# A Hawk and RWKV block on one core: each recurrent gate by fifteen products

## The chip, the cores and the metric

The kernel runs on one core of a Trainium2 chip. The metric is the device time of one execution in microseconds; smaller is better. TensorE multiplies matrices into PSUM, which is eight banks of 128 x 512 numbers here; ScalarE (ACT) applies functions and copies; VectorE (DVE) does element-wise work, scans and statistics; GpSimd (POOL) does element-wise work between SBUF tiles; SyncE (SP) issues DMAs. Each engine works through its own instructions in program order, and waits on semaphores where it needs another's result.

## What is computed

Eight sequences of 1024 tokens with 256 channels go through a layer norm, and a recurrent block (Hawk) and a feed-forward block (RWKV channel mix) are added to the input. Everything is float32.

```python
gate = xn @ Wg.T;  u = xn @ Wi.T                       # 256 -> 384
y  = causal_depthwise_conv(u, conv_w, K=4) + conv_b
ig = sigmoid(y @ lru_Wi.T + lru_bi)                    # 384 -> 384
rg = sigmoid(y @ lru_Wg.T + lru_bg)
alpha = exp(-8 * softplus(lam) * rg)
beta  = sqrt(1 - alpha**2 + 1e-6)
h[t]  = alpha[t] * h[t-1] + (beta * ig * y)[t]
hawk  = (gelu(gate) * h) @ Wo.T                        # 384 -> 256
xr = mu_r * xn + (1 - mu_r) * xn_prev;  xk likewise with mu_k
ffn = sigmoid(xr @ W_r.T) * (relu(xk @ W_k.T)**2 @ W_v.T)
out = x + hawk + ffn
```

## The kernel before

Channels lie on partitions, tokens along the free axis: 384 channels are three chunks of 128, 1024 tokens are two halves of 512, so that one 128 x 512 product fills a PSUM bank. The kernel does not multiply block by block. A 2 x 2 block of weights (two output chunks, two input chunks) times two token halves takes seven products instead of eight. The class `Group` holds such a set. It uses sums of weight blocks, which `weight_sum` makes once on GpSimd, and sums of token blocks, which `token_sum` (L803) makes on GpSimd, four for each matrix that is multiplied. Of a group's steps, `seed` (L491) copies bank A to a new bank B, `five` (L496) copies bank C to SBUF, `fork_c` (L499) and `fork_d` (L507) add B and that copy on VectorE, and `evict` applies the output function. Where a third input chunk exists, each of the four outputs gets one more ordinary product, eleven a group in all.

The groups of a sequence are: u0, u1, u2 (u and gate, 7 products each, L415), k (7, L415), r and v (7 each, by token, L421), o (11, by token, L421), and l0, l1, l2 for the two recurrent gates together (11 each, L415): the six rows of output chunks of both gates are taken as three pairs. A product by token is four instructions of 128 columns. In the last sequence l takes the same chunk of both gates as a pair, and the o products of the last two sequences are done there without groups (L830). In the first sequence u0 and v are plain as well.

Around them, per sequence: VectorE adds three of the four convolution taps (`conv_rest`, L898; the first tap, `conv_first`, is ScalarE's), mixes xk and xr (`mix`, L820), computes layer-norm statistics of the next sequence (L725, L729), transposes its tokens in 32 x 32 squares (L780), which sixteen small DMAs on SP's queue (`spread`) carry to their places; and for the recurrence computes 1 - alpha squared (`decay_rest`, L915), `gated_input` (L922), `scaled_input` (L925), the scan `recur` (L930) and `gated_state` (L934). ScalarE normalizes, evicts, and computes exp, square and sqrt. `add_x` is a DMA on GpSimd's queue that adds x to the sum in `side`.

The order of instructions is laid out by hand. Every step is entered with a time by `at` or `pe`, all steps are sorted by it, and the sorted list is issued. For steps of ScalarE, VectorE, GpSimd and SP the table `PLACES` (four parts: first, second, middle, last sequence) replaces the time by one that a planner found, relative to the start of the sequence; TensorE's products count up a clock of their own in the order in which the loop calls `Group.step`. So the table fixes only an order, and what each engine waits for at run time is the data. Banks are taken from the front of a list of eight and given back at its end.

The recurrence of a sequence runs while the next sequence's u, k and r products are made; its o product comes later in that sequence. The two gates stand at the end of each sequence, and the u products of the next one are interleaved with their last groups.

Of the kernel before, what the change touches and what calls it, by code (L numbers as in the profile page):

```python
# [12 lines left out]
P = 128  # L13
NT = 512
# [22 lines left out]
        "early weight_sum u 0 False": 2.01, "early_put 1": 2.2, "early normalize 4 1": 2.3,  # L37
        "early weight_sum u 2 False": 2.32, "early normalize_on_vector 5": 2.35,
        "early weight_sum u 1 False": 3.04, "early weight_sum u 3 False": 3.59, "early_put 2": 3.62,
        "early normalize 6 1": 3.64, "early normalize_on_vector 7": 3.65, "u0_0 evict 0 0": 3.66,  # L40
        "early parameters": 4.36, "early weight_sum r 2 False": 4.66, "u0_0 evict 1 0": 5.16,
        "early weight_sum r 0 False": 5.38, "early weight_sum k 0 False": 5.75,
        "early weight_sum k 2 False": 6.13, "early weight_sum k 1 False": 6.5, "early load 0 8": 6.86,
        "early_put 3": 6.86, "early weight_sum r 1 False": 6.87, "early weight_sum k 3 False": 7.18,
        "early mix_before k 0": 7.48, "early token_sum x 0": 7.5, "early weight_sum r 3 False": 8.66,
        "early mix_before k 1": 8.7, "early mix k 0": 9.03, "u0_0 evict 1 1": 9.92,
        "early token_sum x 1": 10.53, "u1 seed": 10.86, "u0_0 evict 0 1": 11.55, "early mix k 1": 11.69,
        "u1 five": 12.23, "u2 seed": 12.91, "early token_sum x 2": 13.19, "second stats 1 1": 13.5,
        "conv_first 1": 13.59, "second stats 2 1": 14.23, "early token_sum k 0": 14.35,
        "early mix_before r 0": 14.94, "second stats 6 1": 14.96, "early token_sum x 3": 15.51,  # L50
        "u1 fork_c": 15.86, "u1 evict A 0 0": 16.16, "early token_sum k 1": 16.67,
        "second stats 0 1": 16.67, "u2 five": 16.85, "early mix_before r 1": 17.53,
        "early token_sum k 2": 17.84, "u2 fork_c": 17.86, "second stats 7 1": 18.67, "k seed": 18.86,
        "early token_sum k 3": 19.0, "conv_first 0": 19.55, "early mix r 0": 20.16, "k five": 20.89,
        "u1 fork_d": 21.66, "early token_sum r 0": 21.82, "u1 evict C 0 1": 21.86,
        "second stats 3 1": 22.46, "early halve v": 22.98, "u2 fork_d": 23.19,
        "second stats 4 1": 23.99, "u2 evict A 0 0": 24.04, "early weight_sum l 0 False": 24.71,
        "second stats 5 1": 24.72, "u2 evict C 0 1": 24.73, "k evict A 0 0": 25.41,
        "early constant 16": 25.61, "k fork_c": 25.86, "early constant 0": 26.09,
        "early mix r 1": 26.69, "r seed": 26.86, "early constant 1": 27.54, "u1 late": 27.8,  # L60
        "conv_rest 1 1": 28.18, "r five": 28.48, "conv_first 2": 29.16, "early token_sum r 1": 29.68,
        "u2 evict B 1 0": 30.51, "conv_rest 0 1": 30.84, "u1 evict B 1 0": 31.19, "u2 late": 31.87,
        "early token_sum r 2": 32.34, "k fork_d": 32.34, "early constant 2": 33.49,
        "early token_sum r 3": 33.63, "early weight_sum l 1 False": 33.7, "r fork_c": 33.77,
        "early constant 3": 34.38, "early weight_sum l 3 False": 34.51, "k evict B 1 0": 34.53,
        "early weight_sum l 2 False": 35.77, "r fork_d": 35.86, "k late": 36.28, "conv_rest 2 1": 36.43,
        "conv_rest 1 2": 38.21, "r evict B 1 0": 39.35, "k evict C 0 1": 40.03, "conv_rest 0 2": 40.08,
        "deviation": 40.1, "r evict A 0 0": 41.42, "conv_rest 0 3": 41.48, "inverse 0 8": 41.6,
        "r evict C 0 1": 42.02, "conv_rest 2 2": 42.96, "normalize 4 1": 43.4, "token_sum y 0": 44.45,
        "r late": 44.8, "conv_rest 1 3": 45.6, "l0 seed": 46.8, "conv_rest 2 3": 47.0, "l0 five": 47.65,  # L70
        "normalize 2 1": 47.7, "normalize 7 1": 47.72, "normalize 1 1": 47.74, "normalize 6 1": 48.0,
        "normalize 5 1": 48.29, "value 0": 48.34, "token_sum y 1": 48.34, "normalize 0 1": 48.93,
        "value 6": 49.06, "token_sum y 2": 49.38, "l0 evict A 0 0": 49.72, "value 2": 49.8,
        "normalize 3 1": 50.52, "token_sum y 3": 50.52, "l0 fork_c": 50.86,
        "early weight_sum o 0 False": 51.6, "early weight_sum v 2 False": 51.62,
        "early weight_sum o 1 False": 51.64, "value 4": 51.67, "early weight_sum v 0 False": 51.68,
        "l1 seed": 51.86, "early weight_sum o 2 False": 52.06, "early weight_sum v 1 False": 52.44,
        "early constant 4": 52.82, "add_x": 52.82, "l1 five": 52.86, "early constant 5": 53.14,
        "early constant 6": 53.47, "early constant 7": 53.79, "l0 fork_d": 53.98,
        "early weight_sum v 3 False": 54.65, "early constant 8": 55.03,  # L80
        "early weight_sum o 3 False": 55.21, "early constant 9": 55.59, "l0 evict C 0 1": 55.86,
        "early constant 10": 55.91, "early constant 11": 56.23, "early constant 12": 56.43,
        "put_transposed 0 0": 56.46, "early constant 13": 56.56, "early constant 14": 56.88,
        "put_transposed 1 0": 56.94, "early constant 15": 57.03, "early constant 17": 57.35,
        "put_transposed 0 1": 57.51, "early constant 18": 57.67, "load_for_squares": 57.86,
        "put_transposed 1 1": 58.19, "token_sum x 0": 58.36, "mix_before k 0": 58.88,
        "token_sum x 2": 59.52, "l0 evict B 1 0": 60.1, "mix k 0": 60.68, "mix_before k 1": 60.9,
        "l1 evict A 0 0": 62.13, "token_sum x 1": 62.18, "l1 fork_c": 62.86, "decay 0": 62.93,
        "token_sum k 0": 63.34, "l0 evict D 1 1": 64.27, "mix k 1": 64.5, "l2 seed": 65.07,
        "l2 five": 65.86, "token_sum x 3": 66.0, "mix_before r 0": 66.55, "l1 fork_d": 66.86,  # L90
        "token_sum k 2": 67.17, "mix r 0": 67.6, "mix_before r 1": 67.77, "token_sum k 1": 68.33,
        "l1 evict C 0 1": 69.0, "token_sum k 3": 69.63, "decay_square 0": 69.8, "l2 evict A 0 0": 70.91,
        "l2 fork_c": 71.0, "mix r 1": 71.2, "decay_rest 0": 71.31, "decay 1": 71.71, "stats 1 1": 72.2,
        "stats 6 1": 72.5, "stats 2 1": 72.8, "decay 2": 73.05, "l1 evict B 1 0": 74.39,
        "l1 evict D 1 1": 75.19, "l2 fork_d": 75.92, "decay_square 2": 75.99, "stats 4 1": 76.1,
        "stats 0 1": 76.2, "stats 7 1": 76.72, "decay_square 1": 77.1, "stats 5 1": 77.45,
        "l2 evict C 0 1": 78.21, "stats 3 1": 79.6, "decay_rest 1": 83.35, "decay_rest 2": 86.75
    },
    "second": {
        "token_sum r 0": -0.6, "gated_input 0": 0.68, "u0 seed": 1.51, "token_sum r 2": 2.1,  # L100
        "gated_input 1": 3.27, "beta 0": 3.69, "token_sum r 1": 4.69, "u0 five": 4.92,
        "u0 evict A 0 0": 5.6, "u0 fork_c": 6.66, "token_sum r 3": 6.66, "l2 evict B 1 0": 7.78,
        "scaled_input 0": 7.82, "u1 seed": 8.58, "l2 evict D 1 1": 9.27, "recur 0 L": 10.06,
        "u1 five": 10.07, "k seed": 10.75, "k five": 11.43, "gated_input 2": 11.51, "u0 fork_d": 12.94,
        "beta 1": 13.61, "recur 0 R": 13.74, "u0 evict C 0 1": 14.84, "scaled_input 1": 15.2,
        "u1 evict A 0 0": 15.52, "beta 2": 16.21, "u1 fork_c": 16.62, "k evict A 0 0": 17.43,
        "k fork_c": 17.43, "conv_first 0": 18.12, "gated_state 0": 18.23, "u2 seed": 19.46,
        "scaled_input 2": 19.65, "u0 evict B 1 0": 20.14, "u2 five": 20.83, "token_sum o 0": 21.08,
        "u1 fork_d": 21.36, "deviation": 21.51, "conv_first 1": 21.89, "recur 2 L": 22.24,
        "u1 evict C 0 1": 23.23, "k fork_d": 23.7, "recur 2 R": 24.5, "u1 late": 25.41,  # L110
        "inverse 0 8": 25.96, "k late": 26.1, "conv_rest 0 1": 26.33, "u2 evict A 0 0": 26.78,
        "k evict C 0 1": 27.46, "u2 fork_c": 27.83, "gated_state 2": 28.63, "k evict B 1 0": 29.25,
# [129 lines left out]
def kernel(  # L242
# [211 lines left out]
    def now():  # L454
        return clock[0]
# [907 lines left out]
```

## Time and profile before

| what | value |
|---|---|
| time, median of 3 runs | 619.85 us (619.23 to 619.87) |
| profiled execution: span from first to last instruction | 617.3 us (the page gives no other time for it; 2.6 us below the median) |
| TensorE busy | 611.9 us, 99% |
| VectorE busy | 530.7 us, 86% |
| ScalarE busy | 472.6 us, 77% |
| GpSimd busy | 319.4 us, 52% |
| HBM read and written | 19.94 MB and 8.39 MB |
| granted TensorE clock | 1.000 |

The page shows one execution. Busy time is the union of an engine's instructions; their records overlap by some 0.09 us from one to the next, so the distance between starts is shorter than a record. A float32 product is two records (MATMUL), so a count of 288 is 144 products.

### The profile page before, as it was taken

To read this page: it belongs to the slowest core of one execution; us is meant where nothing else is said; L and a number is where in the kernel's file an instruction comes from. 1 tells how busy PE (TensorE), PEld (TensorE's weight loads), DVE (VectorE), ACT (ScalarE), POOL (GpSimd) and SP (SyncE) were. 2 spreads that over 40 slices of the span, in tenths; PEclk is the share of its full clock that TensorE was granted. 3 is DMA by queue.
4 is the path that set the end of the run, shared out by engine and by line. 5 is a ranking of instruction groups with operands and counts; after the bars stand their busy time and mean duration, and the time that the engine had idled before them with its cause. 6 is when DMAs were issued, how large, how long until landed. Compare 5 with 4: busy or idle time off the path is not lost.

```text
span 617.3 us, 7489 instructions
## 1 busy us (share of the span) xinstructions
PE 611.9 (99%) x2539; PEld 369.8 (60%) x2539; DVE 530.7 (86%) x659; ACT 472.6 (77%) x671; POOL 319.4 (52%) x227
## 2 busy tenths in 40 slices
PE   8999999999999999999999999999999999999997
PEld 5475445954469544794448844497445964457466
DVE  5898798999989788898899888998888986789696
ACT  5988998569894788938888398884898749884880
POOL 4977913578044950649307482085911769427000
PEclk9999999999999999999999999999999999999999
DMA  8201600164002910039000480006500044000403
GB/s 274 67 1 13 124 0 1 31 175 69 0 1 52 202 21 1 0 82 193 0 1 1 102 171 1 1 6 159 110 0 1 18 120 70 0 0 1 70 17 119
DMA packets 35479, 35.10 MB, mean 57 GB/s; under 512 B 2801, under 2 KB 34929, under 8 KB 35441
## 3 DMA queue, kind: packets, MB, share of 16 engines
q1 hardware_dynamic: 26416, 25.63, 15.1%
q0 software_dynamic: 8320, 8.39, 9.2%
q10 hardware_dynamic: 704, 0.60, 0.3%
q8 instruction: 20, 0.33, 0.2%
q14 instruction: 19, 0.15, 0.1%
HBM read 19.94 MB, written 8.39 MB: 46 GB/s over the span
## 4 chain that ended last, share of the span: by engine, by line
PE 96%; DVE 3%; issue 1%; ACT 0%; DVEq 0%
PE bank L415 67%; PE bank L421 22%; PE bank L830 4%; DVE y L898 1%; PE bank L581 1%; PE bank L1025 1%; DVE xk L780 0%; PE bank L1044 0%; DVE bank L499 0%; PE bank L754 0%; DVE q L930 0%; DVE side L507 0%; DVE five L507 0%; DVE bank L507 0%; ACT xt L749 0%
## 5 line engine op out<-in xcount | busy, mean ns | idle before, releaser
L415 PE MATMUL bank<-y,w_l 128*128 128x512 f32 x288 | 138.2, 593 | 0.1
L898 DVE SCALAR_TENSOR_TENSOR y<-u,par,y 128x1024 f32<-128x1024 f32 x72 | 112.5, 1586 | 0.2
L491 ACT COPY bank<-bank 128x512 f32<-128x512 f32 x76 | 43.7, 576 | 60.7 <-PE bank L415 44.9
L415 PEld LDWEIGHTS bank<-y,w_l 128*128 128x128 f32 x288 | 53.0, 190 | 59.2 <-issue 56.6
L499 DVE TENSOR_TENSOR bank<-bank,five 128x512 f32<-128x512 f32 x76 | 52.3, 690 | 26.8 <-PE bank L415 24.9
L415 PE MATMUL bank<-ysum,sum_l 128*128 128x512 f32 x144 | 71.0, 593 | 0.0
L415 PE MATMUL bank<-xsum,sum_u 128*128 128x512 f32 x138 | 69.4, 592 | 0.0
L803 POOL TENSOR_TENSOR tr<-g 128x512 f32<-128x512 f32 x12 | 22.0, 1835 | 83.4 <-ACT u L611 69.4
L803 POOL TENSOR_TENSOR ysum<-y,ysum 128x512 f32<-128x512 f32 x16 | 28.4, 1777 | 53.5 <-DVE y L898 51.0
L803 POOL TENSOR_TENSOR xsum<-ysum 128x512 f32<-128x512 f32 x12 | 15.0, 1270 | 66.0 <-PE bank L421 58.8
L415 PEld LDWEIGHTS bank<-ysum,sum_l 128*128 128x128 f32 x144 | 26.9, 190 | 34.8 <-issue 29.2
L496 ACT COPY five<-bank 128x512 f32<-128x512 f32 x76 | 43.6, 583 | 4.8 <-PE bank L415 2.9
L415 PE MATMUL bank<-xnT,w_u 128*128 128x512 f32 x92 | 47.0, 592 | 0.0
L415 PEld LDWEIGHTS bank<-xsum,sum_u 128*128 128x128 f32 x138 | 25.7, 190 | 29.6 <-issue 26.8
L623 ACT ACTIVATE tr<-bank,half_b 128x512 f32<-128x512 f32 x48 | 31.9, 678 | 14.5 <-PE bank L415 14.4
L421 PE MATMUL bank<-w_o,g 128*128 128x128 f32 x288 | 37.0, 275 | 0.0
L623 ACT ACTIVATE ti<-bank,half_b 128x512 f32<-128x512 f32 x48 | 31.5, 683 | 7.1 <-PE bank L415 6.9
L421 PEld LDWEIGHTS bank<-w_o,g 128*128 128x128 f32 x288 | 35.0, 192 | 2.9 <-issue 2.9
L749 ACT ACTIVATE xt<-xt,mv,std 128x256 f32<-128x256 f32 x60 | 33.9, 597 | 0.9 <-DVE mv L740 0.9
L922 DVE SCALAR_TENSOR_TENSOR ti<-ti,y 128x1024 f32<-128x1024 f32 (+1 forms) x25 | 29.9, 1217 | 3.9 <-ACT ti L623 3.9
L803 POOL TENSOR_TENSOR ysum<-y 128x512 f32<-128x512 f32 x16 | 20.3, 1270 | 23.7 <-DVE y L898 16.3
L925 DVE SCALAR_TENSOR_TENSOR ti<-ti,q 128x1024 f32<-128x1024 f32 (+1 forms) x25 | 31.8, 1272 | 0.7
(165 smaller groups left out, 1476.2 us busy)
## 6 DMA issues: line engine op xcount, KB each, us to landing
side<-in_x_dram POOLq DMA_DIRECT2D x8, 1024.0 KB, 9.3
xt<-in_x_dram SPq DMA_DIRECT2D x28, 256.0 KB, 5.0
xnT<-xk SPq DMA_DIRECT2D x96, 64.0 KB, 2.0
out_dram<-side SPq DMA_DIRECT2D x12, 512.0 KB, 5.2
xt<-in_x_dram SPq DMA_DIRECT2D x1, 1024.0 KB, 5.5
out_dram<-side SPq DMA_DIRECT2D x4, 256.0 KB, 2.2
out_dram<-side SPq DMA_DIRECT2D x6, 128.0 KB, 1.7
w_l<-in_lru_wg_dram SPq DMA_DIRECT2D x1, 576.0 KB, 6.1
```

The costliest lines, as they stand in the source:

```text
L415: nc.tensor.matmul(banks[b], weight, tokens, start=start, stop=True, skip_group_check=True)
L421: nc.tensor.matmul(banks[b][:, p], tokens[:, p], weight, start=start and j == 0, stop=True, skip_group_check=True,)
L491: nc.scalar.copy(banks[bank["B"]], banks[bank["A"]])
L496: nc.scalar.copy(self.five, banks[bank["C"]])
L499: nc.vector.tensor_tensor(banks[bank["C"]], banks[bank["B"]], self.five, ALU.add)
L623: nc.scalar.activation(dst[:, m, HALVES[h]], src, AF.Tanh, bias=half_b[:, b + m : b + m + 1], scale=0.5)
L749: nc.scalar.activation(xa, xa, AF.Identity, bias=m, scale=r)
L803: nc.gpsimd.tensor_tensor(dst[o], a, b, ALU.subtract)
L830: nc.tensor.matmul(banks[b][:, j * D : (j + 1) * D], lhs[:, c, (t + j) * P : (t + j + 1) * P], families[w][:, c, :], start=(j == 0 and c = ...
L898: nc.vector.scalar_tensor_tensor(y[:, m, :], u[:, m, k : k + S], column(COL_CONV_W + k * HC + m), y[:, m, :], ALU.mult, ALU.add,)
L922: nc.vector.scalar_tensor_tensor(ti[:, m, p], ti[:, m, p], 1.0, y[:, m, p], ALU.add, ALU.mult)
L925: nc.vector.scalar_tensor_tensor(ti[:, m, p], ti[:, m, p], 0.5, q[:, m, p], ALU.mult, ALU.mult)
```

## The change

Each recurrent gate is now computed on its own: three output chunks by three input chunks by two token halves, 18 block products, are done by fifteen. Two gates take 30 products a sequence, where l0, l1 and l2 took 33. `gate_weight` makes the fifteen weight operands for both gates at once, in twenty steps (18 on GpSimd, one on ScalarE, one on VectorE) in the first sequence, out of the raw weights, which are loaded into the tile q. `form` makes ten sums of y blocks on VectorE, into the six halves of u (whose values the convolution has used up) and the four parts of ysum; five of the fifteen products take y itself. GpSimd's four sums of y are gone. Partial sums are shared between the outputs through three bank copies (`copy`) and four copies into the output's own place in tr or ti (`keep`), on ScalarE, and five adds (`join`) on VectorE, for each gate.

The order of all engines, TensorE and SP included, now comes from a new table `PLACES` (1,182 entries) with the starts of the sequences in `BASES`; every step has an entry of its own, the products too. The sums for o go to q where they went to tr. The copies `five` take a buffer from a list and give it back. Stores are steps of their own. The groups u, k, r, v and o, the convolution, the recurrence and the output are computed as before.

```diff
-        "l": fixed("w_l", [HC, 2 * HC * P]),
...
-    def l_group(s, gi):
...
+    def gates(name, n, s):
+        dst = (tr, ti)[n]
...
+        rows = {**raw_forms(s), **{i: forms(s)[k] for i, k in FORM_OF.items()}}
...
+        def mm(i, key, new=False):
+            if new:
+                bank[key] = take()
+            product(bank[key], gate_w[:, i, n, :], rows[i], start=new)
+        def copy(key, new):
+            bank[new] = take()
+            nc.scalar.copy(banks[bank[new]], banks[bank[key]])
+        def keep(key, o, h):
+            nc.scalar.copy(place(o, h), banks[bank[key]])
...
+        put("p11", mm, 11, "A", True)
+        put("copy B", copy, "A", "B")
+        put("p0", mm, 0, "A")
+        put("keep 14", keep, "A", 0, 0)
+        put("p4", mm, 4, "B")
+        put("keep 10", keep, "B", 1, 1)
+        put("p10", mm, 10, "A")
+        put("keep 13", keep, "A", 2, 0)
+        put("p3", mm, 3, "B")
+        put("join G", join, "G", "B", "", ALU.subtract, 2, 0)
+        put("p2", mm, 2, "B")
+        put("keep 8", keep, "B", 1, 0)
+        put("join 0", join_last, "", "", "B", ALU.subtract, 0, 0)
+        put("p7", mm, 7, "A")
+        put("copy E", copy, "A", "E")
+        put("p8", mm, 8, "G")
+        put("evict G", evict, "G", 2, 0, 1)
+        put("p14", mm, 14, "A")
+        put("copy F", copy, "A", "F")
+        put("p1", mm, 1, "E")
+        put("evict E", evict, "E", 2, 1, 1)
+        put("p9", mm, 9, "F")
+        put("evict F", evict, "F", 0, 1, 1)
+        put("join A8", join, "A", "A", "", ALU.subtract, 1, 0)
+        put("p12", mm, 12, "A")
+        put("join H", join, "H", "A", "", ALU.add, 1, 1)
+        put("p13", mm, 13, "A")
+        put("evict on", evict_on, "A", 1, 0)
+        put("p6", mm, 6, "H")
+        put("evict H", evict, "H", 1, 1, -1)
+        put("join A0", join, "A", "", "A", ALU.subtract, 0, 0)
+        put("p5", mm, 5, "A")
+        put("evict A", evict, "A", 0, 0, 1)
...
+    def form(s, k):
+        half, f = halves_for("y", s), forms(s)
+        out, a, b, op = (
+            (0, half(1, 0), half(1, 1), ALU.add),
+            (1, half(0, 1), f[0], ALU.subtract),
+            (2, half(0, 0), f[1], ALU.add),
+            (3, f[2], half(2, 0), ALU.subtract),
+            (4, f[3], half(2, 1), ALU.subtract),
+            (5, f[0], half(2, 1), ALU.add),
+            (6, f[5], half(2, 0), ALU.add),
+            (7, f[6], half(0, 0), ALU.subtract),
+            (8, half(1, 1), half(2, 1), ALU.add),
+            (9, f[8], f[7], ALU.subtract),
+        )[k]
+        nc.vector.tensor_tensor(f[out], a, b, op)
...
-        load_weight(nc.sync, "lg", lru_wg)
-        load_weight(nc.sync, "li", lru_wi)
+        for n, src in enumerate((lru_wg, lru_wi)):
+            nc.sync.dma_start(q[:, :, n * HC * P : (n + 1) * HC * P], src)
...
-                token_sums(now() + 1.1, s, "y")
...
+            for k in range(10):
+                at(form, s, k)
+            era[0] = "own" if last else ""
+            for n, name in enumerate(("rg", "ig")):
+                gates(name, n, s)
```

## The prediction

> **What bounds the kernel now.** I read the page's first part, then the chain that ended last for one sequence in the middle, then the busy time by stretch, then VectorE's groups and its order beside GpSimd's.
>
> ```profile
> PE 611.9 (99%) x2539; PEld 369.8 (60%) x2539; DVE 530.7 (86%) x659; ACT 472.6 (77%) x671; POOL 319.4 (52%) x227
> ```
>
> TensorE is busy for all but 5.3 us of the span; VectorE stands at 86%. The chain for 205.7 to 280.4 us (start, length, what), one whole sequence of the steady state:
>
> ```profile
> 205.71 45.49 PE bank L415 x106
> 251.20 1.78 PE bank L421 x16
> 257.35 16.08 PE bank L421 x144
> ```
>
> It holds TensorE and nothing else. Each product is two records, so L415 gives 45.49/53 = 0.858 us per 512-column product, and L421 16.08/144 x 8 = 0.893 us per product by token (four instructions of 128 columns). A sequence has 61 of the first and 25 of the second: 61 x 0.858 + 25 x 0.893 = 74.7 us, the distance between equal points of the chain. Busy time by stretch (window, length, PE, PEld, DVE, ACT, POOL):
>
> ```profile
> 205.70:280.40 74.70, 74.70 (x324) 45.45 (x323) 65.74 (x79) 58.97 (x84) 37.85 (x26) 1.00 0.28 60
> 280.40:355.10 74.70, 74.70 (x323) 45.46 (x323) 65.74 (x79) 57.33 (x83) 38.13 (x26) 1.00 0.24 53
> ```
>
> TensorE is full and VectorE has 9 us to spare in each sequence. That margin is what the change spends. VectorE's groups of one such window, and GpSimd's order in it:
>
> ```profile
> L898 DVE SCALAR_TENSOR_TENSOR y<-u,par,y 128x1024 f32<-128x1024 f32 x9 | 14.1, 1589 | 0.0
> L499 DVE TENSOR_TENSOR bank<-bank,five 128x512 f32<-128x512 f32 x10 | 6.9, 687 | 3.9 <-PE bank L415 3.9
> L820 DVE SCALAR_TENSOR_TENSOR xr<-xnT,par,xr 128x1024 f32<-128x1024 f32 x2 | 3.7, 1840 | 0.0
> L915 DVE TENSOR_SCALAR q<-q 128x1024 f32<-128x1024 f32 x3 | 3.7, 1249 | 0.0
> ```
>
> ```profile
> 334.26 3.91 DVE L898 SCALAR_TENSOR_TENSOR y<-u,par,y 128x1024 f32<-128x1024 f32 x2
> 342.14 1.27 DVE L898 SCALAR_TENSOR_TENSOR y<-u,par,y 128x1024 f32<-128x1024 f32 x1
> 334.83 2.26 POOL L803 TENSOR_TENSOR tr<-g 128x512 f32<-128x512 f32 x1
> 339.26 1.27 POOL L803 TENSOR_TENSOR ysum<-y 128x512 f32<-128x512 f32 x1
> ```
>
> A convolution step takes 1.27 us alone and up to 2.25 beside GpSimd; a GpSimd sum goes from 1.27 to 2.26 likewise. Over the window this lengthens VectorE by 6.7 us: 9 x (1.589 - 1.27) = 2.9 on y, 3 x (1.249 - 0.69) = 1.7 on L915 (0.69 where GpSimd rests), 2 x (1.84 - 1.28) = 1.1 on xr, about 1.0 on others. By the sums beside them: o sums 2.9, r sums 2.8, y sums 0.5, the rest little. The adds that read a PSUM bank (L499, L507) stay at 0.69 with GpSimd busy or not.
>
> **The change, part by part.** *Products.* 33 become 30 in each of 8 sequences: 24 x 0.858 = 20.6 us off the engine that is the chain. The by-token products stay. This gives 619.85 - 20.6 = 599.25 us if nothing else comes due. (The profiled execution spans 617.25, 2.6 below the median; I carry the 2.6 as constant, so the span would be 596.65.)
>
> *VectorE.* A sequence loses 6 adds of the old groups (fork_c, fork_d) and gains 10 joins and 10 sums of y. All are 128x512. In the order of the profile such an add starts the next 0.60 us later (0.69 with overlapping ends). So 14 x 0.60 = +8.4 us: 65.7 + 8.4 = 74.1 against TensorE's new 58 x 0.858 + 25 x 0.893 = 72.1. Summed over the kernel: 530.7 + 112 x 0.60 = 598 us of VectorE against 591.3 of TensorE. This is the term on which everything turns. What comes off: the y sums on GpSimd go, and with them 0.5 us of lengthening. The r sums now follow the second xr mix, where VectorE's order holds joins, evictions from banks and statistics, rows that GpSimd does not lengthen; of their 2.8 us I take 1.0 off, not all, because k sums now run into the three L915. That leaves 72.6, or 0.5 above TensorE. A join also waits in VectorE's queue for its product; behind it stand evictions of o and v, statistics, mixes and the other gate's joins, so a late product holds the banks of o and v too; with two gates interleaved I cost that at nothing, the hand-offs below if not. Bounds: 0 above TensorE (4.6 or less of lengthening left), and 2.0 above if all 6.7 stays. Over the second to the seventh sequence and half the last, 6.5 x 0.5 = 3.3 us.
>
> The trace has no sum of two SBUF halves on VectorE beside a busy GpSimd: its nearest uncovered row, L934 (g times q, 1.22 us for 1024), never met one. The Trainium skill, "SBUF — State Buffer", section "Who interferes with whom", speaks against the change here: a VectorE instruction with two SBUF inputs is locked out for the whole of a GpSimd instruction that reads SBUF, and one with a PSUM input is not. By that rule the ten sums can each wait for a GpSimd sum and the ten joins cannot; if half of the ten waited 1.27 us, an estimate from that page and the row above, the sequence would be 6 us longer on VectorE and the kernel would lose.
>
> *ScalarE.* 48 seed and five copies go, 112 copies come (6 copy and 8 keep a sequence): 64 x 0.52 us between starts = +33, and six table loads fewer (45 to 39 in the order) x 1.28 = -8. 472.6 + 25 = 498 us, 83% of 599: hidden behind TensorE; uncovered, it would add at most the 3 us a sequence of its growth.
>
> *GpSimd.* 32 y sums (48.7 us) and eight sum_l (12.5) go; 18 gate_weight adds of 128x256 come, between the 0.46 of a 128x128 row and the 1.0 (alone) to 1.7 of a 128x384 row: 8 to 30 us, 0.73 x 18 = 13 taken. It falls to about 271 us; no saving by itself. The two gate weight loads move from w_l to q on the same SP queue, at the same place: nothing.
>
> *The first sequence.* There the gates' first product now needs all nine convolution steps and five sums of y; the old one needed two chunks. In the profile the convolution ends at 51.4 and TensorE came to the gates at 48.5. Five sums make 54.4. TensorE now has the four transposes (2.07 us) ahead of the gates: 50.6. So a new wait of 3.8 us on TensorE, with all gate products and the next sequence's u products queued behind it; between 0, if GpSimd's weight sums happen to leave the convolution alone (15.1 us for nine steps there, 4.4 over the uncontended), and 6, if they press harder.
>
> *The tail.* After the last gate products 18 output products of the earlier sequence and 4 of the own stand before the first that needs chunk 2: 36 records and 8 at 18.29/84 = 0.218 us make 9.6. The chain behind the last product (evict, exp, square, table load, sqrt, scan, multiply) took from 595.9 to 605.1 = 9.2 in the profile. Covered by 0.4; at nothing, up to 1.5 if ScalarE comes later.
>
> Everything moved in the new order (spread, loads, stores, statistics) keeps its count. On SP's queue the four loads for the squares move ahead of 13 of the 16 spreads; add_x goes between the o sums of the next sequence on GpSimd's. DMA stood at a quarter of its time in these windows, so I cost it at nothing; spreads held up by those loads would delay mix, by up to the 5.0 us in which such a load lands, once a sequence.
>
> Sum: 619.85 - 20.6 + 3.8 + 3.3 = 606.3 us.
>
> **The rivals.** *All hidden, 599 to 602.* If the new order keeps GpSimd's sums beside the joins and lets most products run ahead, VectorE's 74.1 falls by more than 2 and only the first wait, 0 to 3 us, is left. For it: TensorE did not wait in five whole windows; 11 or 12 of 20 GpSimd sums now stand next to gates. Against: VectorE would be at 98% in step with TensorE at 100%.
>
> *Hand-offs, 612 to 621.* Each gate has seven points where a product reads what ScalarE or VectorE has just put in a bank (three copies, four joins): 14 a sequence where nine were. TensorE's weight loads waited 2.9 us in 7 cases on L499, 0.4 each. If a third of 112 points is uncovered at 0.4: 15 us, 618. Two gates laid between each other speak against it.
>
> *VectorE takes over, 621 to 635.* One mechanism: sums of y and convolution beside the o, v and x sums of GpSimd. From VectorE's 74.1 less 0.5, five of ten sums lengthened by their own 0.6 give 76.6 a sequence, 4.5 over TensorE: 599.25 + 3.8 + 6.5 x 4.5 = 632. It decides from 74.7 a sequence (16.8/6.5 = 2.6 above 72.1); VectorE without any relief stands at 74.1, so little is needed.
>
> That the change does not do what it says is out: the built order has 457 products of 512 columns where 481 were.
>
> **How the numbers follow.** Forecast (602 to 612) 0.40, all hidden 0.22, hand-offs 0.11, VectorE takes over 0.27. A measurement of this kernel tells 0.2%, some 1.2 us, from no change. Faster: 0.40 + 0.22 + half of the hand-offs, 0.68; same 0.04; slower 0.28. The range runs from the floor, 599, to 624: above that lies some 0.17 of the last rival.
>
> **What would show it.** Right: equal points of the chain 72.6 us apart in the middle; VectorE 72 busy of them, with TensorE waiting for y, u or ysum sums of VectorE 0.5 us a sequence; a gap of 2 to 6 us on TensorE near 51 us; joins at 0.69. Wrong: 74.7 or more between the points, sums of y well over 0.7 each, or waits on banks in the gates.

## The result, and the profile after

The changed kernel takes 688.45 us (median of 4 runs, 685.92 to 690.04), beside 619.54 for the kernel before in the same session: a ratio of 1.111, interval 1.1083 to 1.1137. It is slower by a ninth, far outside the range forecast. The profiled execution spans 684.0 us where before spanned 617.25. The first line of the page's part 1, and the row of TensorE's clock in part 2:

```profile
PE 616.4 (90%) x2491; PEld 367.7 (54%) x2491; DVE 584.8 (85%) x772; ACT 493.0 (72%) x730; POOL 265.7 (39%) x205
...
PEclk9999999979999899998999999998999999999999
```

The 48 TensorE records are gone (2539 to 2491), worth 20.6 us, and yet TensorE is busy 4.5 us longer: the clock's row, full throughout before, now dips. By the clock's own records it stood at half for 41 us in all, in stretches that begin within a wait or just behind it. In 31 of these 41 us TensorE was at work, and half of that, some 16 us, is what the half clock cost; the other 9 us of the 25 were not taken apart. The larger part of the loss is idle TensorE: 5.3 us before, 67.6 now. So the span's +66.7 is +62.3 of idle time and +4.5 of busy time.

Busy time by stretch, two middle sequences from one equal point to the next (window, length, PE, PEld, DVE, ACT, POOL, clock, DMA):

```profile
227.88:311.90 84.02, 75.72 (x317) 45.34 (x316) 72.10 (x94) 60.29 (x90) 30.54 (x21) 0.96 0.23 50
311.90:396.75 84.85, 76.48 (x316) 45.51 (x316) 72.43 (x94) 60.29 (x90) 30.89 (x21) 0.96 0.24 51
```

Set against 74.70 before, a sequence is 9 to 10 us longer, though no engine has more than 77 us of work in it. VectorE's need is what the prediction put down (72.1 to 72.4 for 72.6). Its groups in the first of these windows:

```profile
L1122 DVE SCALAR_TENSOR_TENSOR y<-u,par,y 128x1024 f32<-128x1024 f32 x9 | 12.2, 1377 | 0.0
...
L594 DVE TENSOR_TENSOR bank<-bank,five 128x512 f32<-128x512 f32 x7 | 4.6, 687 | 0.1
...
L1139 DVE TENSOR_SCALAR q<-q 128x1024 f32<-128x1024 f32 x3 | 2.3, 760 | 0.7 <-ACT q L1136 0.7
L733 DVE TENSOR_TENSOR bank<-bank,tr 128x512 f32<-128x512 f32 x3 | 2.1, 699 | 6.5 <-ACT tr L725 4.4 <-ACT bank L722 1.8 <-PE bank L531 0.3
```

The joins (L733) take 0.70 each as expected, but VectorE idles 6.5 us in front of these three: what they read comes late. TensorE's waits over the whole execution (who waits <- for whom: us in total, times, longest):

```profile
PE bank L531 <- ACT bank L722: 29.1, 6, 9.4
PE bank L531 <- DVE g L603: 8.9, 5, 3.8
PE bank L537 <- DVE bank L594: 7.7, 6, 1.6
PE bank L531 <- DVE bank L594: 5.1, 6, 1.4
PE bank L531 <- POOL xsum L1022: 4.0, 1, 4.0
```

L722 is ScalarE's copy in the gates. The timeline of one sequence (start, us, instruction, count, [idle before <- releaser]) tells why it is late. TensorE, ScalarE, and SP's queue:

```profile
310.85 1.05 PE L537 MATMUL bank<-w_v,xsum 128*128 128x128 f32 x8
316.80 5.49 PE L531 MATMUL bank<-u,gate_w 128*128 128x512 f32 x6 [4.90 <-ACT bank L722]
322.08 1.48 PE L531 MATMUL bank<-ysum,gate_w 128*128 128x512 f32 x2
323.39 1.02 PE L531 MATMUL bank<-u,gate_w 128*128 128x512 f32 x2
```

```profile
313.48 2.19 ACT L1033 ACTIVATE xr<-xnT,mu_rest 128x1024 f32<-128x1024 f32 x2 [15.06 <-DMA xnT<-xk]
315.57 0.57 ACT L894 ACTIVATE side<-bank 128x512 f32<-128x512 f32 x1
316.17 0.57 ACT L722 COPY bank<-bank 128x512 f32<-128x512 f32 x1
```

```profile
298.42 2.32 SPq L1011 DMA_DIRECT2D xnT<-xk  x3
300.83 2.59 SPq L936 DMA_DIRECT2D xt<-in_x_dram  x4
303.46 8.45 SPq L1011 DMA_DIRECT2D xnT<-xk  x13
```

Read from the bottom: SP issues 16 spreads at 0.65 us each, with the four loads for the squares let in after the third, and is done at 311.9. ScalarE has nothing to do but mix_before of r, which reads what the last spread brings; it stands idle for 15.06 us. Behind it in ScalarE's order stand an eviction of r and the gate's copy B; for copy B waits p0 of the first gate, and so TensorE, 4.90 us. Then six records take 5.49 us, where six take 2.74 at full clock (d2 below). In the second sequence the same chain costs 9.4 us of wait and 10.2 us at half clock.

The trace of before holds the same wait, with nothing behind it that mattered. SP and ScalarE there:

```profile
340.07 11.34 SPq L792 DMA_DIRECT2D xnT<-xk  x16
351.51 2.03 SPq L717 DMA_DIRECT2D xt<-in_x_dram  x4
```

```profile
353.08 2.19 ACT L814 ACTIVATE xk<-xnT,mu_rest 128x1024 f32<-128x1024 f32 x2 [2.62 <-DMA xnT<-xk]
```

There mix_before stood behind the seed and five copies of the first gate group, and the loads behind all the spreads.

### The profile page after: what moved, and what is told of

Same layout as the page of the kernel before. It is cut to its first block, busy times and chain, and to the rows that moved or that the text cites. A ratio compares the mean times of both kernels' runs of the same rounds, so it can differ in the third digit from the quotient of the medians.

```text
span 684.0 us, 7426 instructions
## 1 busy us (share of the span) xinstructions
PE 616.4 (90%) x2491; PEld 367.7 (54%) x2491; DVE 584.8 (85%) x772; ACT 493.0 (72%) x730; POOL 265.7 (39%) x205
## 5 line engine op out<-in xcount | busy, mean ns | idle before, releaser
L531 PE MATMUL bank<-u,gate_w 128*128 128x512 f32 x192 | 103.4, 656 | 29.9 <-ACT bank L722 29.1
L531 PEld LDWEIGHTS bank<-u,gate_w 128*128 128x128 f32 x192 | 38.7, 209 | 77.3 <-issue 37.4
L1033 ACT ACTIVATE xr<-xnT,mu_rest 128x1024 f32<-128x1024 f32 x16 | 17.7, 1140 | 86.4 <-DMA xnT<-xk 86.4
L531 PE MATMUL bank<-y,gate_w 128*128 128x512 f32 x160 | 77.2, 593 | 2.1 <-DVE bank L733 2.1
L531 PE MATMUL bank<-ysum,gate_w 128*128 128x512 f32 x128 | 65.6, 598 | 1.0 <-DVE bank L733 0.6
L1022 POOL TENSOR_TENSOR xsum<-xnT 128x512 f32<-128x512 f32 x16 | 23.8, 1489 | 88.2 <-DMA xnT<-xk 63.1
L531 PEld LDWEIGHTS bank<-y,gate_w 128*128 128x128 f32 x160 | 30.0, 190 | 39.6 <-issue 33.3
L733 DVE TENSOR_TENSOR bank<-bank,tr 128x512 f32<-128x512 f32 x24 | 16.6, 694 | 38.6 <-ACT tr L725 26.6
L531 PEld LDWEIGHTS bank<-ysum,gate_w 128*128 128x128 f32 x128 | 24.3, 193 | 33.7 <-issue 23.7
L1022 POOL TENSOR_TENSOR q<-g 128x512 f32<-128x512 f32 x12 | 16.2, 1349 | 66.7 <-DVE g L1158 59.7
L594 DVE TENSOR_TENSOR bank<-bank,five 128x512 f32<-128x512 f32 x52 | 35.0, 688 | 8.1 <-PE bank L531 5.6
L722 ACT COPY bank<-bank 128x512 f32<-128x512 f32 x48 | 27.7, 581 | 19.2 <-PE bank L531 18.4
L1154 DVE TENSOR_TENSOR_SCAN q<-tr,q,ti 128x512 f32<-128x512 f32 x23 | 35.5, 1542 | 0.1
L1022 POOL TENSOR_TENSOR rsum<-xr 128x512 f32<-128x512 f32 x8 | 10.5, 1316 | 62.6 <-DVE xr L1039 62.6
```

Of the source, the lines that this page charges most:

```text
L531: nc.tensor.matmul(banks[b], weight, tokens, start=start, stop=True, skip_group_check=True)
L594: nc.vector.tensor_tensor(banks[bank["C"]], banks[bank["B"]], held["five"], ALU.add)
L722: nc.scalar.copy(banks[bank[new]], banks[bank[key]])
L733: nc.vector.tensor_tensor(got, a, b, op)
L1022: nc.gpsimd.tensor_tensor(dst[o], a, b, ALU.subtract)
L1033: nc.scalar.activation(mixes[which][:, c, :], xnT[:, c, X0 - 1 : X0 - 1 + S], AF.Copy, scale=mu_rest[:, n : n + 1])
```

## The experiments

All times are medians beside a median of 618.9 to 620.0 for the kernel before on the same chip. Edits to the order are changes of one number in PLACES, shown as "old > new". The letters of the theories are used anew from the second group on. In e6, e7 and e8 one sum of r, in the last sequence, is taken ahead of the mix that it reads (in e6 also one of k in the first); no instruction is more or fewer for it. From e9 on the base is e8 with that sum put back behind its mix; this base has no run of its own.

### 1. The queue behind the spreads

**e1_mix_late**: mix_before behind the gates' first copies, as before had it.

```diff
 middle: mix_before r 0 50.593 > 54.88, r 1 50.593 > 54.89, k 0 52.275 > 54.90
         mix r 1 56.186 > 57.60, mix r 0 56.526 > 57.61, mix k 0 57.493 > 57.62
 second: mix_before r 1 65.436 > 73.87, k 1 66.717 > 73.88, r 0 69.580 > 73.89; mix r 1 76.654 > 77.663
```

> The changed kernel with one edit: in the second and the middle sequences ScalarE does mix_before behind the gates' first copies and keeps instead of ahead of them, and VectorE its mix behind the first joins. Theory A (ScalarE's queue stands behind mix_before, which waits for the last spread; the bank copy behind it holds TensorE 4.9 us a sequence, 9.4 in the second, and the clock then falls to 0.5 for 6.8 to 10.2 us): the gap and the low clock go, 4.9 + 3.4 us in five sequences and some 14 in the second, about 50 us: 630 to 645. Rival B (VectorE, busy 72.1 us a sequence, has taken over): joins come as late as before, 675 or more. Rival C (hand-offs in the gates): the gap moves to a later copy or join, 665 to 685.

666.29 us, above theory A's range: TensorE's waits for copy B (L722) fall from 29.1 to 3.0, but 9.4 us turn up on the keeps (L725) that now stand behind mix_before on ScalarE, up to 4.0 us in the second sequence. That is the outcome named for rival C, by theory A's chain. **e2_loads_last**: the loads behind the spreads.

```diff
 middle: load_for_squares 38.873 > 47.5      second: load_for_squares 60.271 > 62.5
```

> The changed kernel with one edit on SP's queue: the four loads for the squares are issued after all sixteen spreads, as in the kernel before. Theory A: the last spread comes 2.0 us earlier, the gap before the gates goes from 4.9 to about 2.8 us, the low clock from 6.8 to 3.4 us or nothing: 3.8 to 5.5 us in each of five sequences and some 2 in the second, 655 to 670. Rivals B and C: no change beyond 1%, 680 or more.

666.66 us, in range; TensorE's waits for L722 fall from 29.1 to 15.0. **e3_both**: both edits.

> Both edits together. Theory A: no gap before the gates, period 84 to about 75.5 us (72.1 of products and 3.3 of the three small waits on VectorE's fork adds), TensorE busy near 592 us; 622 to 640 with the start as it is. Rival B: 675 or more. Rival C: 665 to 685.

662.11 us. Either edit gives 22 us, both 26: they cut the same chain. A middle sequence falls to 79.1, not to the 75.5 expected, so something else is left.

**b1_mix_early**: the kernel before, with two mix_before of k put ahead of the first gate group's seed, and nothing else.

```diff
 middle: mix_before k 0 > 54.30, mix_before k 1 > 54.31     (l0 seed follows)
```

> The kernel before with one edit: in the middle sequences ScalarE does both mix_before of k ahead of the seed copy of l0 instead of behind it. Theory A: the seed comes some 6 us later (it waits for the last spread and two mixes), TensorE waits 3 to 5 us in each of five sequences and the clock falls for 3.4 to 6.8 us: 4.5 to 8 us a sequence, 642 to 660. If order on ScalarE does not matter beside VectorE's load (rival B): 620 to 625, since VectorE has 9 us to spare here.

646.78 us: 28 us slower, ratio 1.0457 (1.0427 to 1.0488), with 17.8 us of TensorE's waits, in five cases, on a seed copy that the old kernel never waited for, and a mean clock of 0.986. One place in one queue, without any of the change's arithmetic, makes a loss of the same kind. This cause is shown from both sides. It is worth some 26 of 69 us.

### 2. Places of single steps, and VectorE's load

**e4_adds_early**: e3_both with six moves on VectorE.

```diff
 middle: u2 fork_d 31.381 > 30.55, conv_rest 1 2 37.739 > 39.80, gated_state 0 15.790 > 16.1417
 second: u2 fork_c 40.806 > 40.743, conv_rest 0 2 50.801 > 51.93      last: r fork_c 28.206 > 26.970
```

> e3_both plus six moves on VectorE's queue alone: in the middle sequences u2's fork_d goes ahead of the scan recur 2 R, the convolution step 1 2 goes behind the fork_c of o and v, gated_state 0 goes behind u1's fork_c; in the second u2's fork_c ahead of recur 1 R and conv_rest 0 2 behind r's fork_c; in the last r's fork_c ahead of form 0. No work is added or taken. Theory A (what is left in e3_both, 662.1 us, is the order in which single adds stand in a queue): the three gaps of 1.28, 1.26 and 0.71 us close in five middle sequences, 3.8 us each with the slower products around them, 19 us, and 3 us more in the second and the last: 637 to 645 us, the points of a middle sequence 75.3 apart. Theory B (VectorE's load of 73 us a sequence sets the pace, and a place in the queue only shifts the gap): 656 us or more, period 78 to 79, with the gaps turned up behind other adds.

657.96 us. The three gaps of each sequence closed, and four of 0.4 to 0.6 us opened behind other adds, a seed and an eviction; a sequence went from 79.1 to 78.4. That is theory B's outcome.

**e6_all**: more moves of that sort, on ScalarE, GpSimd and VectorE.

```diff
 middle: mix_before r 0 > 52.95, r 1 > 56.00, k 0 > 56.01 (between the gate copies); v evict C, o evict D > 57.492
         mix r 0 > 58.9, mix k 0 > 63.77, gated_state 2 > 34.487
 second: mix_before r 1, k 1 > 74.135, r 0 > 77.75, k 0 > 78.44; mix r 0 > 77.76
 first:  halve v, weight_sum r 2, k 3, r 3, v 0, gate_weight 11, 0, 1 behind token_sum x 0; three constants behind ig join G
```

> e4_adds_early plus: ScalarE's four mix_before set singly between the gate copies instead of three in a row, the evictions of v and o ahead of the mixes on VectorE, the squares 2 us earlier; at the start x's first sum ahead of halve v, three weight sums and three gate_weight steps on GpSimd; in the first sequence three constants behind a join. No work is added or taken. Theory A: 2.0 us a middle sequence from the copies and evictions (10), the 5.4 us gap at the start and its 6.8 us at half clock (8.8), 2 gaps of 2.1 to 2.3 us with 3.4 us at half clock each (7): 610 to 620 us, below or at the kernel before. Theory B (VectorE's load): 630 us or more, with VectorE busy for over 97% of a middle sequence.

649.86 us, 77.1 for a middle sequence: a time that theory B allowed, but without its sign. VectorE was busy 94% of it, not 97, and most of its idle time lay in one place, among the joins.

**e7_fold**: 3.4 us a sequence less on VectorE.

```diff
-            at(decay_rest, m)                       # VectorE: q = 1 - q
-    activation(q, q, AF.Sqrt, bias=beta_eps)
+    activation(q, q, AF.Sqrt, bias=beta_eps, scale=-1.0)     # beta_eps = 1 + 1e-6
```

> e6_all (whose first sequence takes one sum of k ahead of the second mix of k, put right here) without the three decay_rest steps a sequence on VectorE: the 1 - a*a is folded into the square root on ScalarE (scale -1, bias 1 + 1e-6), the same function. That takes 3 instructions of 0.69 to 1.25 us, 3.4 us a sequence with what GpSimd adds to them, from VectorE and nothing from another engine. In e6_all VectorE had no idle time for 44 us of each 77 (convolution, scans, adds, sums of y) and TensorE's seven small gaps lie in or behind that stretch. Theory B (VectorE's load in this stretch holds TensorE back): a middle sequence falls from 77.1 to 74 us, the kernel from 649.9 to 625 to 632. Theory A (order of single steps alone): 645 to 650.

646.77 us. VectorE's load over the sequence fell by 3.4 us and the time by 0.4 a sequence, so as a load over the whole sequence it doesn't set the pace. The text above took the three steps for part of the stretch in which VectorE never rests; in e6 they stand at 320.5 to 324.8 us, among the joins (the gates run from 292.8 to 329.2), where it does. **e8_fold_order**: more moves on top.

```diff
 first:  gate_weight 11, 0, 1, 19, 2 behind token_sum r 3; mix k 0 > 58.787
 second: scaled_input 2 > 44.70; stats 3, 4 behind rg join G; stats 7, 5, 1 behind ig join G
 middle: scaled_input 2 > 26.275, normalize 4, 2 > 27.735, gated_state 2 > 39.797, conv_rest 1 3 > 42.412
```

> e7_fold with more moves: at the start five gate_weight steps behind r's sums on GpSimd (in e6_all r's sums kept TensorE 4.2 us, and the clock at half for 3.4); in the second sequence two statistics that wait for a load behind the first join, three more behind the second, and scaled_input 2 behind u2's fork_d; in the middle scaled_input 2 behind u1's fork_d, two normalizations behind u2's first eviction, gated_state 2 and conv_rest 1 3 behind the adds of o. No work is added or taken. Theory A: 5.9 us at the start, 4 us in the second sequence, 1.5 to 2 us in each of five middle ones, 17 us or so below e7_fold. Theory B: 8 us or less below e7_fold, since in the saturated stretch a place in the queue only shifts the gap.

646.44 us. The small gaps are gone, and a sequence is as long as it was: they have run together into one, in front of the first gate product. TensorE in a middle sequence, and the first of its waits:

```profile
371.60 1.99 PE L531 MATMUL bank<-u,gate_w 128*128 128x512 f32 x4 [2.55 <-DVE u L814]
```

```profile
PE bank L531 <- DVE u L814: 14.7, 7, 4.3
```

L814 is the sums of y. In the sequence shown one of them met a GpSimd sum and took 1.79 us for 0.69; where none did, in three of the five middle sequences, the wait is 1.45 us. That gave the third theory: VectorE is short in one stage.

### 3. VectorE by stage

The windows view, cut at the first and the last gate product of a middle sequence. Two rows each (between two gate stages; within the gates), before and after:

```profile
232.58:273.26 40.68, 40.68 (x226) 28.95 (x225) 37.86 (x39) 30.76 (x50) 14.13 (x9) 1.00 0.07 18
273.26:307.27 34.01, 34.01 (x99) 16.49 (x98) 27.88 (x42) 27.57 (x34) 24.00 (x16) 1.00 0.48 104
```

```profile
267.54:309.12 41.58, 38.32 (x230) 28.45 (x229) 41.29 (x44) 27.75 (x45) 14.16 (x9) 1.00 0.35 67
309.12:352.15 43.03, 38.13 (x89) 17.07 (x88) 30.82 (x51) 32.54 (x46) 18.20 (x13) 0.92 0.23 51
```

Between the gates VectorE went from 37.86 of 40.68 us to 41.29 of 41.58: it is full there, and TensorE, with 38.3 us of work, waits. Within the gates it has 12 us free. In e8 it is still busy for 39.85 of 40.90 us between the gates, and idles 6.8 of 35.32 within them.

**e9_taps_out** and **e10_mixes_out** take work from VectorE on the two sides of that border.

```diff
 e9   for k in range(1, K):  >  range(1, K - 1):  at(conv_rest, m, k)     # 3.8 us between the gates
 e10  mix(which, c):  scalar_tensor_tensor(...)  >  pass                  # 5.1 us within the gates
```

> e8_fold_order (with r's sums of the last sequence behind r's mix) without the last of the three convolution steps of each chunk: 3 x 1.27 us a sequence less on VectorE, between one sequence's gates and the next one's; its output leaves those taps out. Theory C (VectorE is short by stage, not by sequence: between two gate stages, 41 to 42 us, it has 0.2 to 1.0 us idle and TensorE waits 1.9 to 3.0; within the gates, 35 us, it idles 6.8): TensorE's wait for the sums of y ends, a middle sequence falls from 77.3 to 74.3 to 75, the first loses its 4.3 us wait and half a 6.8 us stretch at half clock: 620 to 630 us. Theory A (places of single steps): 638 or more.

> The same base without the four second halves of the mixes of r and k: 4 x 1.28 us a sequence less on VectorE, all within the gate stage; its output leaves that part of r and k out. Theory C: VectorE idles there already, so no more than 5 us: 641 to 647 us, with a middle sequence at 76.5 to 77.3. Theory B (VectorE's load over the sequence sets the pace): more than e9_taps_out gains, since 5.1 us are taken in place of 3.8: 612 to 625 us.

622.34 and 650.24 us, beside 646.4 for e8. The smaller relief, between the gates, gives 24 us; the larger one, within them, gives nothing (it came out 3 us above its range, with one sequence at 81.5). The same two rows for e9 and then e10:

```profile
243.00:281.36 38.36, 38.07 (x231) 28.53 (x229) 37.00 (x41) 27.91 (x46) 12.36 (x9) 1.00 0.27 50
281.36:317.09 35.73, 35.33 (x89) 15.62 (x88) 28.95 (x48) 32.23 (x45) 20.16 (x13) 1.00 0.34 76
```

```profile
249.74:290.83 41.09, 38.97 (x231) 28.72 (x229) 40.04 (x44) 28.10 (x46) 13.17 (x9) 1.00 0.28 52
290.83:326.89 36.06, 35.14 (x87) 15.89 (x88) 24.79 (x44) 31.74 (x45) 17.48 (x13) 1.00 0.42 89
```

In e9 TensorE sets the first stage's length (38.07 of 38.36); in e10 VectorE, with 40.04 of 41.09, still does.

**e13_no_sums_of_y** leaves out the change's own ten sums from the second sequence on.

```diff
     def form(s, k):
-        nc.vector.tensor_tensor(f[out], a, b, op)
+        if s == 0:
+            nc.vector.tensor_tensor(f[out], a, b, op)
```

> The base of e9_taps_out (all convolution steps in) without the ten sums of y on VectorE from the second sequence on; the gates' products read what stands in those places, so its output is not the gates' of y. Theory C: 6 to 7 us a sequence go from VectorE's full stretch; TensorE's wait for the first gate product (1.5 to 2.5 us) ends and no new one comes: a middle sequence at 72.5 to 74 us, the kernel at 616 to 624, beside 622.3 without three convolution steps. If something else fills the stretch: 635 or more.

632.73 us: 14 us gained, not the 22 to 30 expected. In the middle the wait is gone and a sequence takes 74.5, a little above its range; the first sequence, which keeps its sums, keeps its wait of 3.4 us and as much at half clock, and a wait of 2.4 us on a late fork_d stayed in the sixth. So without the ten sums the stage is no longer full, but hand-offs of 0.1 to 0.4 us add up to 2.3 us a sequence over TensorE's 72.1.

**e11_k_late** moves 1.7 us of TensorE's work over the border.

```diff
 middle: k mm 0 8.228 > 12.69, k mm 1 8.815 > 12.70, k seed 12.618 > 12.71     (behind ig p5)
```

> The same base with two of k's products (1.7 us of TensorE) moved in the middle sequences from the end of the gate stage to just behind its last product. No work is added or taken. Theory C: the gate stage ends 1.7 us sooner, VectorE's full stretch starts sooner, and TensorE fills with them what it waited: 1.0 to 1.7 us a middle sequence, 637 to 642 us. Against it: the joins of the gates lose the cover of two products, and the kernel stays at 645 to 649.

648.88 us, no gain. In the fourth sequence the gate stage took 33.7 us for 35.3 in e8, the stage behind it 42.6 for 42.0, and the wait stayed at 1.9 us in the mean of the five. This would fit a full stretch of VectorE that does not start with TensorE's last gate product; no run shows what starts it.

**e12_sums_gpsimd** puts five of the ten sums back on GpSimd.

```diff
-        nc.vector.tensor_tensor(f[out], a, b, op)
+        (nc.gpsimd if s > 0 and k > 4 else nc.vector).tensor_tensor(f[out], a, b, op)
 middle: token_sum x 2 45.879 > 51.34
```

> The same base with one part of the change undone in part: sums 5 to 9 of y, from the second sequence on, on GpSimd (1.27 us each for 0.60 to 0.72 on VectorE). That takes 3.0 us a sequence from VectorE's full stretch and adds 6.4 to GpSimd, idle there for 12 us. Theory C without contention: 2.5 us a sequence, 627 to 632 us. Theory C with sums 1 to 4 on VectorE lengthened by 0.6 each beside them: 638 to 644. If the five sums come too late for the gates' third products: 648 or more, with TensorE waiting for ysum on GpSimd.

677.5 us, a time that only the last case allowed for (648 or more), but not by its way: TensorE didn't wait for GpSimd's sums. VectorE's sums, and GpSimd's beside them:

```profile
295.50 2.87 DVE L815 TENSOR_TENSOR u<-y,u 128x512 f32<-128x512 f32 x2
298.41 3.30 DVE L815 TENSOR_TENSOR u<-u,y 128x512 f32<-128x512 f32 x2
```

```profile
296.23 1.59 POOL L815 TENSOR_TENSOR ysum<-ysum,y 128x512 f32<-128x512 f32 x1
297.90 1.60 POOL L815 TENSOR_TENSOR u<-ysum,y 128x512 f32<-128x512 f32 x1
```

Four sums of 0.70 us became 1.44 and 1.65 each in the mean of a pair, and the chain to the first gate product 3.3 us longer than with four undisturbed ones; its wait rose to 4.8 us in five sequences, each followed by 6.8 us at half clock. Sums 5 to 9, which came off VectorE, stand behind that chain in its order.

### 4. The half clock

**d1_spare_products**: the changed kernel with four products by a weight of zeros in the second gate, meant to run within the wait.

```diff
+        def spare():
+            for i in range(4):
+                product(bank["A"], zero, rows[8])
```

> The changed kernel as it was given (688.4 us), with four products by a weight of zeros (3.4 us of TensorE, they add nothing to their bank) put into TensorE's order in the five middle sequences where it waits 2.1 to 5.0 us for the gate's copy B. Theory D (an idle TensorE loses its clock, and runs at half for one or two stretches of 3.4 us afterwards): the wait shrinks to 1.5 us or less, the stretches at half clock behind it (6.8, 6.8, 6.8 or 3.4, 3.4) go, half of them is won back, and where the wait was under 3.4 us up to 1.3 are lost: 672 to 682 us. If the half clock has nothing to do with the wait: 688 to 692 us with the same stretches in the clock's row.

704.58 us: 16 us more. The product that waits is p0 of the first gate, and these stood behind it; the waits and the half clock stayed. It tells nothing of the clock. **d2_spare_ahead**: the same four ahead of p0.

> As d1_spare_products, but with the four products (3.4 us, a weight of zeros) ahead of the product that waits, p0 of the first gate, so that they run within the wait. Theory D (the half clock follows TensorE's idle time): what is left of the wait is 1.6 us or less in the three sequences with 4.9 to 5.0 us of it and none in the two with 2.1 and 2.8, where 0.6 to 1.3 us are lost; the stretches of 6.8, 6.8, 3.4 and 3.4 us at half clock behind these waits go, half of each won back, 10 us, less the 2: 678 to 682 us beside 688.4. If the half clock has another cause (the gate products themselves, the chip's heat): 688 to 692, with the same stretches in the clock's row.

681.72 us, ratio 1.1008 (1.0964 to 1.1052), 6.7 us less than without, for 17 us of added products. The same place as in the timeline above:

```profile
311.59 2.74 PE L531 MATMUL bank<-y,zero 128*128 128x512 f32 x6
314.17 1.05 PE L537 MATMUL bank<-w_v,xsum 128*128 128x128 f32 x8
317.02 2.84 PE L531 MATMUL bank<-u,gate_w 128*128 128x512 f32 x6 [1.79 <-ACT bank L722]
```

The six gate records that took 5.49 us behind the wait now take 2.84. Of the four stretches at half clock behind the copy in the middle none is left. The untouched waits near 18, 140 and 455 us are followed by theirs still, and two waits of 2.1 and 2.2 us that had none have one here. So the half clock follows from idle time, not from the gate products, which are the same in both.

## Why the prediction was wrong, point by point

*Products: right.* 48 records fewer, at an unchanged 0.43 us spacing at full clock.

*VectorE's need, ScalarE, GpSimd: right in size.* 72.1 to 72.4 us a sequence for 72.6; joins 0.70 for 0.69; 493 for 498; 265.7 for 271. That VectorE's sum came out so close is in part luck, since the lengthening by GpSimd moved: a convolution step took 1.38 us where 1.59 was carried over, while g times q went from 1.22 to 1.57 and the second halves of the scans from 1.27 to 1.62.

*The step that failed first: "Everything moved in the new order ... I cost it at nothing".* The text named the loads moved ahead of 13 spreads and priced them by DMA's busy share and by the landing time of a load, 5.0 us. It even gave the delay of mix, "up to the 5.0 us", but followed it no further. Neither is the price. A spread costs SP's queue 0.65 to 0.7 us of issue, 16 of them 11 us, and the four loads 2.6 more; and the text did not see that mix_before, which waits for the last spread, had been moved ahead of the gate's copy B on ScalarE. e1, e2, e3 and b1 put this at 22 to 28 us.

*The second: VectorE's 72.6 against TensorE's 72.1, taken over a sequence.* The excess of 0.5 us a sequence was worked out from an average of two stages with different limits. Between the gates VectorE needs 41.3 us against 38.3; within them it has time to spare. Priced from the stage, the term would have been some 3 us a sequence instead of 0.5; e9 and e10 show that only work on the near side of the border counts. The rival "VectorE takes over" had the right engine, but its mechanism, GpSimd beside the sums of y, was rare: eight of the 80 sums met GpSimd at work, at most one in a middle sequence, and took 0.95 to 1.64 us; the others took 0.7. e12 shows what that mechanism costs when it is made to happen.

*Hand-offs: the sign, not the mechanism.* Waits on banks in the gates came, but as six waits of up to 9.4 us on one copy; on the joins (L733) TensorE waited 2.9 us in three cases. Small hand-offs are what is left in e13, but of its 2.3 us a sequence only 0.3 lie in the gates.

*The third: nothing in the sum for TensorE's clock.* The trace of before, at full clock, couldn't show it; the changed kernel lost some 16 us to it, so that a wait from about 2 us up often cost more than its own length.

*The first sequence: the wait was there, but hidden.* A wait of 3.8 us near 51 us was forecast. In the changed kernel an earlier one, 4.0 us at 18.6 (x's first sum stands behind weight sums on GpSimd, L1022 in the waits), took its place; with that out of the way, e8 shows 4.3 us at 50.9. The tail, at nothing with a bound of 1.5, cost 2.2 us of wait.

*Where the 688 went.* Queue of spreads 26 us (e3); places of single steps, the start among them, 12 (e6); the fold 3 (e7); work on VectorE between the gates up to 24 (e9, by leaving three convolution steps out). Of what is left of 622 over the floor of 599, some 11 us lie in the middle sequences (73.6 to 75.6 us for 72.1); the rest, in the first, the second and the last two, was not taken apart. No version here with all of the work in it beat the kernel before.

On the rule weighed in the prediction ("SBUF — State Buffer", "Who interferes with whom", of the Trainium skill): the traces agree with it where the two met. One sum of y and the GpSimd sum beside it in the changed kernel:

```profile
313.27 1.64 DVE L814 TENSOR_TENSOR ysum<-ysum,u 128x512 f32<-128x512 f32 x1
312.89 1.47 POOL L1022 TENSOR_TENSOR xsum<-xnT 128x512 f32<-128x512 f32 x1 [15.78 <-DMA xnT<-xk]
```

It ends 0.55 us after the GpSimd sum that was under way when it began. In e12 the 25 sums of y that were lengthened, from the second sequence on, all do the same. Since they begin in the middle of a GpSimd sum, 0.5 to 0.95 us are added to each, not the whole of one.

## What to carry to other kernels

When an order is laid out anew, list for every instruction that waits for a DMA what stands behind it on its own engine, and count the queue's issue time, not only the transfer. Work out each engine's need between the points where the engines must meet, stage by stage; a spare tenth over the whole period is worth nothing in a stage that is full. Closing small gaps one at a time only shows the true limit if they stop moving: here they ran together into one wait, and that named the stage.

## What the runs showed of the hardware

TensorE's clock falls to half in stretches of 3.4 us or multiples of it (3.4, 6.8, 10.2) behind its waits. Over all the profiles here, none of 179 waits of 0.7 to 1.8 us was followed by one, 27 of 50 from 1.8 to 3.6 us were, and all 36 above. The Trainium skill, "TensorE: Matmul & The Clock Gate", "Part 1: The HAM clock gate", has the half rate come after an idle window of some 3.4 us and go after a busy one as long; the length agrees with the 3.4 us here, while waits as short as 1.84 us set it off too. Over the changed kernel it was 41 of 684 us, 31 of them with TensorE at work.
